# A four-direction scan and a layer of routed experts on one core: the steps beside a scan are split between the two ends of its turn, and the experts' tiles run in one stretch in the scheduler's order

## The chip, the cores and the metric

The kernel runs on one core of a Trainium2 chip. The metric is the device time of one execution in microseconds; the lower, the better. It was run three times before the change. One further execution was recorded by the hardware profiler, and all durations of single instructions come from that one. PE is the TensorE matmul unit, DVE VectorE, ACT ScalarE, POOL GpSimd and SP the engine that issues most of the DMAs.

## The reference, cut to what matters

Four images of 256 channels and 32x32 pixels pass through two layers. Each layer is a mixer and a layer of experts. The first layer (attention, then eight experts that all see every token) is not concerned here. The second layer is:

```python
# mixer: a selective scan in four directions, 16 states per channel
delta = softplus(xn @ W_delta + b_delta)          # xn: layer norm of the features
dA    = exp(delta[..., None] * -exp(A_log))       # decay per channel and state
dBx   = (delta * xn)[..., None] * (xn @ W_B)      # input per channel and state
h[l]  = dA[l] * h[l - 1] + dBx[l]                 # along rows forth, rows back, columns forth, columns back
y     = sum over states of h * (xn @ W_C), + xn * D, added to x; mean of the directions

# experts: a layer norm, a router, the best 2 of 8 experts for every token
logits = xn @ Wr + br;  top 2, softmax of the two
out    = x + sum of the two: w * (gelu((xn * ln_g[e] + ln_b[e]) @ W1[e] + b1[e]) @ W2[e] + b2[e])
```

There are 4 x 1024 tokens, so 8192 rows for the experts (each token goes to two), and the hidden size of an expert is 1024.

## The kernel before, in words

Tensors of the mixer lie as 128 channels (partitions) by 1024 pixels, two such halves for an image. The scan of one image, one half and one of 16 states is a unit; there are 128 of them, in the order image, half, state. A function `turn(k)` writes out, by hand, the instructions of one turn, which serves several units at different points of their way; inside a manual schedule, each engine gets its instructions in the order in which the code issues them. In turn k:

- at its beginning `for step in steps: next(step, None)` runs one step of the side work (below);
- for unit k+2 SP issues the loads of two broadcast rows (`rows`);
- for unit k+1 ACT computes the decays along the columns (L1514); when that unit is the first of a half, DVE first runs a running sum `cum` over delta (L1609), from which ACT makes `prod` (`products`);
- for unit k-1 POOL multiplies `prod` by the incoming column state (L1560, writes `da_c`), and PE adds that;
- for unit k DVE scans along the rows forth (L1540) and back (L1549), each over 128x1024; PE adds both into a sum in PSUM (`hp`, L1535); POOL takes a small difference `gap`;
- ACT computes the row decays of unit k+1 (L1522), POOL its inputs `uu` (L1527);
- if there is one, POOL issues an indirect DMA that sends 128 tokens to their places for the experts (L1288);
- DVE multiplies the two halves of unit k-1's sum by a row (`yc`, L1576), PE adds them into y, and the last state of a half adds y to x (L1580);
- DVE runs a short scan `come` of 32 steps (L1555);
- a second `for step in steps: next(step, None)` runs another step of the side work;
- DVE scans along the columns (L1566), PE adds.

The side work is written as generators, which stop at each `yield`. `Prep.steps()` prepares the next image: layer norm (L1400 on), the products with W_B and W_C, and for each of four quarters the softplus (L1481 to L1489: `sp`, with ACT's exponentials and logarithms in between) and `rest` (L1457, L1458: delta times the input, and the part with D). `norm(b)` and `route(b)` compute the experts' layer norm, the router's logits, the best two experts, and the place of every token among its expert's rows; `scatter(b)` then sends the tokens (L1288). A turn takes a step at its beginning and one at its end, so the number of `yield`s between two groups of instructions decides at which of the two a group falls. In the kernel before the groups with VectorE work fall at a turn's beginning.

The first three images are routed beside the scans. The last one, image 3, is known only when the scans have ended, so its routing runs beside the experts. There, `Tile` is the work on 256 rows of one expert: `slots` loads the rows (L1665), `weights` loads W1, W2, the biases and the layer norm's factors (L1670 to L1680), `inputs` transposes on PE (`tp`, L1688), scales on DVE (`xe`, L1691) and computes the places of the results (`to`, L1694, a pool of 8 buffers), `hidden` is the first matmul (`hp`, L1703) with ACT's Gelu (`hid`, L1705), `result` the second (`yp`, L1711), a bias on DVE (`ys`, L1714) and two indirect DMAs from POOL that put the rows where they belong (L1716). The 17 `early` tiles are full of rows of the first three images. Their order is written by hand in a manual schedule, with the routing of image 3 in between (`beside`); `hp` and `yp` have two PSUM buffers each. The other tiles are `late`: 19 as a rule, in the scheduler's order, with three `hp` and two `yp` buffers. More of them are written into a branch ahead of these 19, taken only when the counts need it (L1771); in the profiled execution it is not taken. At the end the two results of each token are read back, weighted, transposed and added to x (L1783 to L1795).

Of the kernel before, what the change touches and what calls it, by code (L numbers as in the profile page):

```python
# [11 lines left out]
F32 = mybir.dt.float32  # L12
# [9 lines left out]
P = 128  # L22
# [36 lines left out]
def metaformer(ctx: ExitStack, tc: tile.TileContext, t: dict, out: bass.AP):  # L59
# [1129 lines left out]
    def route(b, space, psum, tag):  # L1189

        used = 0
        yield
# [35 lines left out]
        yield  # L1228
        flat = both.rearrange("p n e -> p (n e)")
# [7 lines left out]
        nc.vector.tensor_copy(place, sums[:, 0].rearrange("p n e -> p e n"))  # L1237
        nc.vector.tensor_scalar(m1, m2, 1.0, None, ALU.add)
# [4 lines left out]
        yield  # L1243
        yield
# [48 lines left out]
    def norm(b, pool, psum, tag, raw_tag, d):  # L1293
# [32 lines left out]
        def rsqrt(dst):  # L1326

            nc.scalar.activation(sd, ve, AF.Sqrt)
            yield
            yield  # L1330
            nc.vector.reciprocal(r0, sd)
            nc.vector.tensor_tensor(sd, r0, r0, ALU.mult)
            nc.vector.tensor_tensor(sd, sd, ve, ALU.mult)
            nc.vector.tensor_scalar(sd, sd, -0.5, 1.5, ALU.mult, ALU.add)
            nc.vector.tensor_tensor(dst, r0, sd, ALU.mult)


        yield
# [7 lines left out]
        nc.vector.tensor_tensor(s2, s2, s1, ALU.mult)  # L1346
        for n in range(NT):
            nc.scalar.mul(tok[:, n, :C], tok[:, n, :C], s2[:, n : n + 1])
# [3 lines left out]
    with ExitStack() as st:  # L1352
# [34 lines left out]
        class Prep:  # L1387
# [9 lines left out]
            def steps(self):  # L1397
# [28 lines left out]
                yield  # L1426
# [4 lines left out]
                nc.vector.tensor_tensor(rs, r0, rr, ALU.mult)  # L1431
                yield
# [29 lines left out]
                for c in range(CT):  # L1462
                    for h in range(NHALF):
                        cols = ts(h, HALF)
                        zp = ps_m.tile([P, HALF], F32, tag="hp", name="zp")
                        for k in range(CT):
                            nc.tensor.matmul(zp, wd[:, k, ts(c, P)], xm[:, k, cols],
                                             start=(k == 0), stop=(k == CT - 1))
                        yield
                        dd = self.delta[:, c, cols]  # L1470
                        sp = p1.tile([P, 4 * HALF], F32, tag="sp", name="sp")
                        v, up, ln, ru = (sp[:, ts(i, HALF)] for i in range(4))
                        nc.scalar.activation(dd, zp, AF.Relu, bias=bd[:, c : c + 1])
                        nc.scalar.activation(v, zp, AF.Abs, bias=bd[:, c : c + 1])
                        nc.scalar.activation(v, v, AF.Exp, scale=-1.0)
                        if last is not None:
                            rest(*last)
                        last = c, cols
                        yield
                        yield  # L1480
                        nc.vector.tensor_scalar(up, v, 1.0, None, ALU.add)  # L1481
                        nc.scalar.activation(ln, up, AF.Ln)
                        nc.scalar.activation(ru, ln, AF.Exp, scale=-1.0)
                        nc.vector.scalar_tensor_tensor(v, up, 1.0, v, ALU.subtract, ALU.subtract, reverse1=True)
                        yield
                        yield
                        nc.vector.tensor_tensor(v, v, ru, ALU.mult)
                        nc.vector.tensor_tensor(v, v, ln, ALU.add)
                        nc.vector.tensor_tensor(dd, dd, v, ALU.add)  # L1489
                        yield  # L1490
                yield
                rest(*last)
# [103 lines left out]
        def turn(k):  # L1596
# [52 lines left out]
    with ExitStack() as st:  # L1649
# [70 lines left out]
        with ExitStack() as sa:  # L1720
# [3 lines left out]
            ps_h = sa.enter_context(tc.tile_pool(name="m1_ps_h", bufs=2, space=PSUM))  # L1724
            ps_y = sa.enter_context(tc.tile_pool(name="m1_ps_y", bufs=2, space=PSUM))
            with tc.manual_schedule():
                todo = [Tile(early, i, "xa", EARLY) for i in range(EARLY)]
                for i in range(EARLY):
                    todo[i].slots()
                    if i < 2:  # L1730
                        todo[i].weights()
                b = B - 1
                routing = chain(norm(b, pa, psa, "t", "raw", pa.tile([P, CT, L], F32, tag="nm_d", name="nm_d")),
                                route(b, pa.tile([P, NUMBERS], F32, tag="numbers", name="numbers"), psa, "t"))
                sending = scatter(b)

                def beside():
                    for _ in range(2):
                        if next(routing, "end") == "end":
                            next(sending, None)  # L1740

                next(routing)
                todo[0].inputs(ps_t)
                for i in range(EARLY):
# [8 lines left out]
                for _ in chain(routing, sending):  # L1753
                    pass

        def run(which):
            with ExitStack() as sb:
                ps_t = sb.enter_context(tc.tile_pool(name="m1_ps_t", bufs=2, space=PSUM))
                ps_h = sb.enter_context(tc.tile_pool(name="m1_ps_h", bufs=3, space=PSUM))
                ps_y = sb.enter_context(tc.tile_pool(name="m1_ps_y", bufs=2, space=PSUM))  # L1760
                for i in which:
                    one_tile = Tile(late, i)
                    one_tile.weights()
                    one_tile.slots()
                    one_tile.inputs(ps_t)
                    one_tile.hidden(ps_h)
                    one_tile.result(ps_y)

        more_tiles = nc.values_load(extra[0:1, 0:1], min_val=0, max_val=1,
                                    skip_runtime_bounds_check_because="a comparison gives 0 or 1")  # L1770
# [96 lines left out]
```

## Time and profile before

| what | us |
|---|---|
| three runs | 4603.13, 4604.02, 4629.91; median 4604.02 |
| the profiled execution | 4608.16 |
| its span, from the first to the last instruction | 4606.1 |
| attention and the first experts | 0 to 2505 |
| preparation of the first image | 2505 to 2557 |
| the scans, 128 turns | 2557 to 3905; DVE busy 1243.3, PE 1247.3, ACT 917.2, POOL 639.6 |
| early tiles, 17 | 3905 to 4251; PE busy 287.8, DVE 46.6 |
| between early and late tiles | 4251 to 4263; PE busy 0.8 |
| late tiles, 19 | 4263 to 4556; PE busy 278.0, DVE 33.7 |
| the last sums | 4556 to 4606; PE busy 15.8, DVE 24.1 |

The page gives each engine's busy time, and under it one digit for each fortieth of the span, the busy share in tenths. A group's row names line, engine, operation, output and input with their shapes and the number of instructions; after the first bar come busy time (us) and the mean of one (ns), after the second the idle time of the engine just before them and what ended most of it. In a timeline the columns are start, duration, engine, line and operation; a bracket tells how long the engine was idle before and what released it. A row of waits names the waiting group, what ended the wait, then the sum in us, the number and the longest. An instruction that was started but could not proceed counts as busy, so a contended operation shows as a long one and not as a wait.

### The profile page before, as it was taken

Reading aid. Unit: us, or ns where it says so; the run is one execution under the profiler, and the core shown is the slowest. Engines: PE = TensorE matmul, PEld = TensorE weight load, DVE = VectorE, ACT = ScalarE, POOL = GpSimd, SP = SyncE. Lnnn points to the kernel's source line nnn. Section 1 sums busy time; section 2 is a strip of 40 time slices with the busy share of each in tenths; the row PEclk is TensorE's granted clock in tenths of the full one; section 3 lists DMA queues with packets and bytes.
Section 4 is the critical chain, followed back from the end, with each engine's and each line's share of the span. In section 5 each row is a group of like instructions: output and inputs, shape, how many; then the busy total and the mean of one; then the engine's idle time right before and its main releaser. Section 6 shows DMA issues by size and latency. Waiting matters only on the chain. (4 is left out here: it accounts for less than half of the span.)

```text
span 4606.1 us, 51252 instructions
## 1 busy us (share of the span) xinstructions
PE 3933.2 (85%) x18522; PEld 2160.5 (47%) x18522; DVE 3137.6 (68%) x5121; ACT 2887.2 (63%) x3788; POOL 1632.1 (35%) x1257
## 2 busy tenths in 40 slices
PE   7478878887888887689999789999999989887996
PEld 4143434443444443366665333433433434666785
DVE  3788899898989898422223799899899898110112
ACT  3989999999899899231112676767767755221222
POOL 0255445555554555310000344445445445011110
PEclk9568877887788788879999899999999999899997
DMA  9200000000000000100000223223333334444555
GB/s 288 56 1 1 10 1 1 1 10 1 1 1 10 1 1 10 38 1 0 0 1 11 84 97 110 101 97 113 102 98 112 104 103 122 150 147 129 184 182 183
DMA packets 171770, 306.81 MB, mean 67 GB/s; under 512 B 27753, under 2 KB 116594, under 8 KB 171506
## 3 DMA queue, kind: packets, MB, share of 16 engines
q1 hardware_dynamic: 161184, 284.10, 19.7%
q0 software_dynamic: 6528, 17.90, 1.0%
q8 instruction: 150, 2.46, 0.2%
q10 hardware_dynamic: 3794, 1.42, 0.1%
q14 instruction: 114, 0.93, 0.1%
HBM read 246.68 MB, written 56.69 MB: 66 GB/s over the span
## 5 line engine op out<-in xcount | busy, mean ns | idle before, releaser
L543 POOL TENSOR_SCALAR dr<-s_n,last 128x1024 bf16<-128x1024 f32 x256 | 728.8, 2864 | 882.3 <-DVE state L571 379.4
L459 ACT ACTIVATE junk_a<-s_n,state 128x1024 int8<-128x1024 f32 x448 | 514.6, 1149 | 23.9 <-DVE state L577 8.2
L1705 ACT ACTIVATE hid<-hp,b 128x256 f32<-128x256 f32 x288 | 134.2, 474 | 466.2 <-PE hp L1703 461.6
L463 DVE TENSOR_SCALAR_CACHE_REDUCE junk_v<-s_n,state 128x1024 int8<-128x1024 f32 x320 | 408.7, 1277 | 8.8
L1560 POOL TENSOR_TENSOR da_c<-prod,come 128x1024 f32<-128x1024 f32 x128 | 261.5, 2043 | 412.7 <-DVE h L1566 362.4
L1114 DVE SCALAR_TENSOR_TENSOR acc<-y,tk_comb,acc 128x256 f32<-128x256 f32 x256 | 120.9, 484 | 349.7 <-PE y L1112 344.1
L510 DVE SCALAR_TENSOR_TENSOR w<-s_n,win 128x1024 f32<-128x1024 f32 x256 | 349.6, 1366 | 5.2
L1703 PE MATMUL hp<-xe,w 128*128 128x256 f32 x1152 | 291.1, 403 | 65.2 <-ACT hid L1705 44.6
L1535 PE MATMUL hp<-h,twice 128*128 128x512 f32 x512 | 253.2, 618 | 91.0 <-DVE h L1540 90.8
L611 ACT ACTIVATE ex<-sT 128x1024 f32<-128x1024 f32 x256 | 247.0, 1015 | 122.5 <-PE sT L603 122.4
L513 DVE MAX8 win<-w 128x8 f32<-128x1024 f32 x256 | 314.5, 1228 | 8.9
L1527 POOL TENSOR_TENSOR uu<-dx,bb 128x1024 f32<-128x1024 f32 x128 | 304.2, 2377 | 40.5 <-DVE dx L1457 40.5
L1107 ACT ACTIVATE hid<-hp,b 128x512 f32<-128x512 f32 x128 | 88.0, 688 | 345.5 <-PE hp L1105 344.7
L459 ACT ACTIVATE junk_a<-s_n,guess 128x1024 int8<-128x1024 f32 x256 | 294.1, 1149 | 7.4
L621 PE MATMUL o_ps<-ex,vT 128*32 128x256 f32 x2048 | 249.8, 458 | 51.5 <-ACT ex L611 41.1
L1540 DVE TENSOR_TENSOR_SCAN h<-da,uu 128x1024 f32<-128x1024 f32 x128 | 291.2, 2275 | 2.7 <-ACT da L1522 2.7
L1566 DVE TENSOR_TENSOR_SCAN h<-da_c,uu 128x1024 f32<-128x1024 f32 x128 | 289.8, 2264 | 0.0
L1549 DVE TENSOR_TENSOR_SCAN h<-da,uu 128x1024 f32<-128x1024 f32 x128 | 289.6, 2262 | 0.0
L1703 PEld LDWEIGHTS hp<-xe,w 128*128 128x128 f32 x1152 | 217.7, 198 | 132.5 <-ACT hid L1705 77.3
L1522 ACT ACTIVATE da<-delta,a_log 128x1024 f32<-128x1024 f32 x128 | 142.8, 1115 | 211.4 <-DVE h L1549 211.4
L1514 ACT ACTIVATE da_c<-delta,a_log 128x1024 f32<-128x1024 f32 x128 | 268.3, 2096 | 0.1
L1112 PE MATMUL y<-w,hid 128*128 128x256 f32 x1024 | 262.9, 394 | 0.0
(517 smaller groups left out, 8209.5 us busy)
## 6 DMA issues: line engine op xcount, KB each, us to landing
bb<-bc_d SPq DMA_DIRECT2D x128, 512.0 KB, 5.0
cb<-bc_d SPq DMA_DIRECT2D x128, 512.0 KB, 4.2
w<-in_w SPq DMA_DIRECT2D x36, 1024.0 KB, 5.1
w2e<-in_w SPq DMA_DIRECT2D x36, 1024.0 KB, 5.6
slots_x<-zeros SPq DMA_DIRECT2D x1, 33282.0 KB, 128.4
y<-results SPq DMA_DIRECT2D x8, 1024.0 KB, 7.2
xs<-slots_x SPq DMA_DIRECT2D x19, 258.0 KB, 5.6
b2e<-in_b SPq DMA_DIRECT2D x36, 128.0 KB, 5.4
```

The costliest lines, as they stand in the source:

```text
L459: nc.scalar.activation(junk, self.row(r), AF.Sign, bias=thr, scale=-1.0, accum_out=u)
L463: nc.vector.tensor_scalar(junk, self.row(r), thr, None, ALU.is_lt, ALU.add, accum_out=u)
L510: nc.vector.scalar_tensor_tensor(w, self.row(r), self.win[:, r, 0:1], self.row(r), ALU.is_gt if r < LAST_DVE else ALU.is_ge, ALU.subtract, ...
L513: nc.vector.max(out=self.win[:, r, 1:], in_=w)
L543: ins = nc.gpsimd.tensor_scalar(dr, self.row(r), self.last[:, r : r + 1], None, ALU.is_lt)
L1112: nc.tensor.matmul(y, hid[:, f, ts(i, P)], w2[:, e, f, :], start=(f == 0), stop=(f == CT - 1))
L1514: nc.scalar.activation(grid(self.da_c), cols_flipped(self.prep.delta[:, self.c]), AF.Exp, scale=self.decay)
L1527: nc.gpsimd.tensor_tensor(self.uu[:, 0], self.prep.dx[:, self.c], self.bb, ALU.mult)
L1540: nc.vector.tensor_tensor_scan(rows.rearrange("p r w -> p (r w)"), self.da, self.uu[:, 0], 0.0, ALU.mult, ALU.add)
L1549: nc.vector.tensor_tensor_scan(hs[:, ::-1], self.da[:, ::-1], self.uu[:, 0][:, ::-1], 0.0, ALU.mult, ALU.add)
L1566: nc.vector.tensor_tensor_scan(hs, self.da_c, self.uu[:, 1], 0.0, ALU.mult, ALU.add)
L1703: nc.tensor.matmul(hp[:, f % 2], self.w1[:, c, ts(f, P)], self.xe[:, c], start=(c == 0), stop=(c == CT - 1))
```

## The change

Three things are done.

1. In the side work, `yield`s are moved, so that VectorE's steps with both inputs in SBUF fall at the end of a turn and those that read PSUM at its beginning. `rest` of a quarter follows the next quarter's matmuls at once.
2. The running sum `cum` of a half is issued one turn earlier, after the second step of a turn and ahead of its columns scan.
3. Early and late tiles are in one stretch without a manual schedule: each early tile is `inputs`, `hidden`, `result`, with six steps of the routing of image 3 after it (the routing and its scatter as one chain), and the scheduler sets the order. `hp` has three buffers, `yp` one. The branch with more late tiles stands after the 19, no longer ahead of them.

```diff
     def route(b, space, psum, tag):
         used = 0
-        yield
...
         nc.vector.tensor_tensor(both, hot1, hot2, ALU.add)
         yield
+        yield
...
         nc.vector.tensor_copy(place, sums[:, 0].rearrange("p n e -> p e n"))
+        yield
         nc.vector.tensor_scalar(m1, m2, 1.0, None, ALU.add)
...
         nc.vector.memset(keep[:, :, 0:1], 0.0)
-        yield
-        yield
         nc.vector.tensor_tensor_scan(cum.rearrange("p e n -> p (e n)"), keep.rearrange("p e n -> p (e n)"),
...
         def rsqrt(dst):
+            yield
             nc.scalar.activation(sd, ve, AF.Sqrt)
-            yield
             yield
...
-        yield
         nc.vector.tensor_scalar(ve, var, 1e-5, None, ALU.add)
...
         nc.vector.tensor_tensor(s2, s2, s1, ALU.mult)
+        yield
         for n in range(NT):
...
                 nc.scalar.activation(sd, ve, AF.Sqrt)
                 yield
-                yield
                 nc.vector.reciprocal(r0, sd)
...
                 nc.vector.tensor_tensor(rs, r0, rr, ALU.mult)
+                yield
                 yield
...
+                        if last is not None:
+                            rest(*last)
+                        last = c, cols
                         yield
...
                         nc.scalar.activation(v, v, AF.Exp, scale=-1.0)
-                        if last is not None:
-                            rest(*last)
-                        last = c, cols
-                        yield
                         yield
                         nc.vector.tensor_scalar(up, v, 1.0, None, ALU.add)
+                        nc.vector.scalar_tensor_tensor(v, up, 1.0, v, ALU.subtract, ALU.subtract, reverse1=True)
+                        yield
                         nc.scalar.activation(ln, up, AF.Ln)
                         nc.scalar.activation(ru, ln, AF.Exp, scale=-1.0)
-                        nc.vector.scalar_tensor_tensor(v, up, 1.0, v, ALU.subtract, ALU.subtract, reverse1=True)
-                        yield
                         yield
                         nc.vector.tensor_tensor(v, v, ru, ALU.mult)
                         nc.vector.tensor_tensor(v, v, ln, ALU.add)
                         nc.vector.tensor_tensor(dd, dd, v, ALU.add)
                         yield
+                        yield
+                rest(*last)
                 yield
-                rest(*last)
                 yield
...
             if 0 <= k + 1 < len(order):
-                b, c, s = order[k + 1]
-                if s == 0:
-
-                    cum = p1.tile([P, L], F32, tag="cum", name="cum", bufs=2)
-                    nc.vector.tensor_tensor_scan(cum, inner, preps[b].delta[:, c], 0.0, ALU.mult, ALU.add)
                 scans[k + 1].column_decays()
...
                 for step in steps:
                     next(step, None)
+            if 0 <= k + 2 < len(order) and order[k + 2][2] == 0:
+
+                b, c, _ = order[k + 2]
+                cum = p1.tile([P, L], F32, tag="cum", name="cum", bufs=2)
+                nc.vector.tensor_tensor_scan(cum, inner, preps[b].delta[:, c], 0.0, ALU.mult, ALU.add)
+            if 0 <= k < len(order):
                 scans[k].columns()
...
-            ps_h = sa.enter_context(tc.tile_pool(name="m1_ps_h", bufs=2, space=PSUM))
-            ps_y = sa.enter_context(tc.tile_pool(name="m1_ps_y", bufs=2, space=PSUM))
-            with tc.manual_schedule():
...
-                next(routing)
-                todo[0].inputs(ps_t)
-                for i in range(EARLY):
-                    todo[i].hidden(ps_h)
-                    beside()
-                    if i + 1 < EARLY:
-                        todo[i + 1].inputs(ps_t)
-                    todo[i].result(ps_y)
-                    if i + 2 < EARLY:
-                        todo[i + 2].weights()
-                    beside()
...
-        with tc.If(more_tiles > 0):
-            run(range(USUAL - EARLY, NTILE - EARLY))
-        run(range(USUAL - EARLY))
+            ps_h = sa.enter_context(tc.tile_pool(name="m1_ps_h", bufs=3, space=PSUM))
+            ps_y = sa.enter_context(tc.tile_pool(name="m1_ps_y", bufs=1, space=PSUM))
+
+            def run(one_tile):
+                one_tile.inputs(ps_t)
+                one_tile.hidden(ps_h)
+                one_tile.result(ps_y)
...
+            for i in range(EARLY):
+                run(todo[i])
+                if i + 2 < EARLY:
+                    todo[i + 2].weights()
+                for _ in range(6):
+                    next(routing, None)
...
+            run_late(range(USUAL - EARLY))
...
+            with tc.If(more_tiles > 0):
+                run_late(range(USUAL - EARLY, NTILE - EARLY))
```

The lines after the change are nearly all one less than before (L1540 is L1539), `cum` is L1636, the branch L1758, and the last sums begin at L1769.

More of the change, by code (lines that the diff above doesn't have):

```diff
@@ L1723, in metaformer @@
             ps_t = sa.enter_context(tc.tile_pool(name="m1_ps_t", bufs=2, space=PSUM))
-            ps_h = sa.enter_context(tc.tile_pool(name="m1_ps_h", bufs=2, space=PSUM))
-            ps_y = sa.enter_context(tc.tile_pool(name="m1_ps_y", bufs=2, space=PSUM))
-            with tc.manual_schedule():
-                todo = [Tile(early, i, "xa", EARLY) for i in range(EARLY)]
-                for i in range(EARLY):
[L1729 to L1740, printed above, removed]
-                next(routing)
-                todo[0].inputs(ps_t)
-                for i in range(EARLY):
-                    todo[i].hidden(ps_h)
-                    beside()
-                    if i + 1 < EARLY:
-                        todo[i + 1].inputs(ps_t)
-                    todo[i].result(ps_y)
-                    if i + 2 < EARLY:
-                        todo[i + 2].weights()
-                    beside()
-                for _ in chain(routing, sending):
-                    pass
@@ L1756, in run @@
[L1756 to L1760, printed above, removed]
+            ps_h = sa.enter_context(tc.tile_pool(name="m1_ps_h", bufs=3, space=PSUM))
+            ps_y = sa.enter_context(tc.tile_pool(name="m1_ps_y", bufs=1, space=PSUM))
@@ new lines, in run @@
+            def run(one_tile):
+                one_tile.inputs(ps_t)
+                one_tile.hidden(ps_h)
+                one_tile.result(ps_y)
+            todo = [Tile(early, i, "xa", EARLY) for i in range(EARLY)]
+            for i in range(EARLY):
+                todo[i].slots()
+                if i < 2:
+                    todo[i].weights()
+            b = B - 1
+            routing = chain(norm(b, pa, psa, "t", "raw", pa.tile([P, CT, L], F32, tag="nm_d", name="nm_d")),
+                            route(b, pa.tile([P, NUMBERS], F32, tag="numbers", name="numbers"), psa, "t"), scatter(b))
@@ L1761, in run, with run_late @@
+            for i in range(EARLY):
+                run(todo[i])
[3 more added lines that the diff above has]
+                    next(routing, None)
+            assert next(routing, "end") == "end"
+            def run_late(which):
                 for i in which:
@@ L1764, in run @@
                     one_tile.slots()
[L1765 to L1770, printed above, removed]
-        with tc.If(more_tiles > 0):
-            run(range(USUAL - EARLY, NTILE - EARLY))
-        run(range(USUAL - EARLY))
+                    run(one_tile)
+            run_late(range(USUAL - EARLY))
+            more_tiles = nc.values_load(extra[0:1, 0:1], min_val=0, max_val=1,
+                                        skip_runtime_bounds_check_because="a comparison gives 0 or 1")
+            with tc.If(more_tiles > 0):
+                run_late(range(USUAL - EARLY, NTILE - EARLY))
         with ExitStack() as sc:
```

## The prediction

> **What bounds the kernel now.** I read the page's parts 1 and 2 first, then the busy time by stretches, then DVE's groups with shapes kept apart, the timeline of one turn, and PE's waits in the experts' stage.
>
> ```profile
> PE 3933.2 (85%) x18522; PEld 2160.5 (47%) x18522; DVE 3137.6 (68%) x5121; ACT 2887.2 (63%) x3788; POOL 1632.1 (35%) x1257
> PE   7478878887888887689999789999999989887996
> ...
> DVE  3788899898989898422223799899899898110112
> ```
>
> The averages mislead: a digit is 115 us, and by stretches the span falls into attention to 1900, the first experts to 2505, preparation to 2557, the scans to 3905, the second experts to 4556 and the sums to 4606. No edit touches anything ahead of 2505, so 2505 us stay. In the scans DVE is busy 1243 of 1348 us and PE 1247: both look full. The rows tell which of them has slack in it (DVE, 2540 to 3905; after the bar the busy time and the mean ns of one):
>
> ```profile
> L1488 DVE TENSOR_TENSOR sp<-sp 128x512 f32<-128x512 f32 x15 | 29.7, 1980 | 0.5
> L1484 DVE SCALAR_TENSOR_TENSOR sp<-sp 128x512 f32<-128x512 f32 x15 | 29.5, 1964 | 0.5
> L1458 DVE SCALAR_TENSOR_TENSOR x<-xm,dskip,x 128x512 f32<-128x512 f32 x12 | 28.8, 2401 | 0.0
> L1487 DVE TENSOR_TENSOR sp<-sp 128x512 f32<-128x512 f32 x15 | 10.0, 665 | 4.7 <-ACT sp L1483 4.7
> ```
>
> L1487 and L1488 are the same operation on the same shape, 665 against 1980 ns. The timeline says why (start, us, engine):
>
> ```profile
> 2687.69 0.66 DVE L1487 TENSOR_TENSOR sp<-sp 128x512 f32<-128x512 f32 x1
> 2687.91 2.21 POOL L1560 TENSOR_TENSOR da_c<-prod,come 128x1024 f32<-128x1024 f32 x1 [3.15 <-DVE h L1566]
> 2688.38 2.29 DVE L1488 TENSOR_TENSOR sp<-sp 128x512 f32<-128x512 f32 x1
> 2690.71 0.69 DVE L1489 TENSOR_TENSOR delta<-delta,sp 128x512 f32<-128x512 f32 x1
> ```
>
> POOL's L1560 starts beside the step, L1488 begins at 2688.38 and ends only after L1560 has ended; L1489, with POOL done, takes 0.69. So the busy time of DVE holds hidden waits.
>
> [...] after a 3.48 us idle, three groups of eight matmuls at 4012.9 to 4026 took 3.78 us instead of 1.99, while after 11.2 us of idle only about 2 us were slow.
>
> **The change, part by part: scans.** A turn on DVE is: first call of the step, forth scan, back scan, two output products, the short scan, second call, columns scan. Start to start an empty turn takes 2.18+2.18+1.18+0.13+2.18 = 7.85 us. L1560 starts 0.1 to 0.2 us after the columns scan, so the first call stands exactly beside it; the second call starts 5.6 us into the turn, when POOL's product L1527 (done by about 4.95) is over and POOL waits for the columns scan. In before all step work falls into the first call. The order of instructions of the changed kernel has the SBUF-only work in the second call, the PSUM readers (L1304, L1317, L1408, L1421, L1441, L1236, L1237) in the first. Removed, as excess over the uncontended duration:
> - per quarter of a preparation L1488 1.60 (2.29−0.69), L1484 1.59, L1458 1.71; 12 quarters run inside turns: 12 × 4.90 = 58.8 us;
> - routing: L1333 6×1.60 = 9.6, L1209 8.6, L1247 5.1, L1257 4.4, L1238 2.9, L1429 1.6, L1168 1.3: 33.5 us.
>
> Together 92.3. What comes back: a quarter's three turns took 10.78+10.51+11.50 = 32.79 and fall to 27.89; PE needs 5 groups of 4 half-matmuls a turn, 8.58 us, and 1.72 for the quarter's zp: 27.46 in three turns. DVE still sets the pace, but with 0.4 us to spare. I charge 4 us for turns where PE becomes the bound (the row of waits already has yc on PE's hp with 18.3 us), 4 us for the PSUM readers of two routed batches that now wait for PE (1.2+0.55+0.15 for a batch, twice), and 1.3 for the layer norm's first factor. The scan cum (L1609, about 2.2 us, 8 times) is only moved, to the second call; DVE pays the same, and ACT's products no longer wait for it, which is off the path (ACT fills 6.3 of 7.85 us). The step's DMA of bc keeps its place; the two row loads per turn on SP too. Net **83 us** (bounds 65: PE binds in most heavy turns; 92: nothing comes back).
>
> **Experts.** Before, an early tile waits four times for ACT, since hp has two buffers; a late tile, with three, does not (PE's waits, us, count, longest; then PE's timeline):
>
> ```profile
> PE hp L1703 <- ACT hid L1705: 44.6, 68, 3.5
> PE hp L1703 <- DVE xe L1691: 20.0, 19, 5.6
> PE tp L1688 <- DMA xs<-slots_x: 11.2, 1, 11.2
> ```
>
> ```profile
> 4182.58 1.99 PE L1703 MATMUL hp<-xe,w 128*128 128x256 f32 x8 [0.61 <-ACT hid L1705]
> ...
> 4281.47 7.17 PE L1703 MATMUL hp<-xe,w 128*128 128x256 f32 x32 [0.80 <-DVE xe L1691]
> ```
>
> A steady early tile takes 17.63 us, a late one 15.33 (hp 7.19, yp 6.92, tp 0.43, wait 0.80). After, hp has three buffers everywhere, and the order shows two tiles' tp together, so one wait for two tiles: 14.95. The 11.2 us for xs, when SP's first late loads stood behind the branch, go too: those loads need only the last slot scatter, long landed by then.
>
> But the scheduler's order adds a wait. `to` (8 buffers) of tile i waits until the result scatters of tile i−8 have landed, and on DVE to(12) now stands ahead of ys(5), xe(6), xe(7); to(13) ahead of ys(6); to(14) ahead of ys(7), xe(8), xe(9). PE waits for these. The scatters wait for each other on POOL and are mixed with batch 3's 16 slot scatters, which become ready after tile 3:
>
> ```profile
> 4120.36 0.96 POOL L1288 DMA_INDIRECT slots_x<-tok,slot  x1 [0.30 <-issue]
> 4125.13 0.96 POOL L1288 DMA_INDIRECT slots_x<-tok,slot  x1 [3.80 <-DMA slots_x<-tok,slot]
> 4128.35 0.96 POOL L1288 DMA_INDIRECT slots_x<-tok,slot  x1 [2.26 <-DMA slots_x<-tok,slot]
> ```
>
> From 4120.36 to 4162.59 there are 13 steps of both kinds, 3.25 us each. With T3 the end of tile 3's yp, the first slot is ready about 7 us later (estimate from the durations of the routing's small operations), and landing takes 3.7. Tile 4's second result is the 8th of that chain and lands at T3+33.5, tile 5's (16th) at T3+59.5, tile 6's (22nd) at T3+7+21×3.25+3.7 = T3+79. Tile 8 can start about 1.7 us later, at T3+80.7, against 4×14.95 = 59.8 unhindered: a loss of 21 us, in three stalls of about 5, 5 and 11. They may bring half rate; a spell cost 3×1.79 = 5.4, and I take one and a half, 8 us. T3 comes at 4000 (in before's time), 8.4 ahead of its 4008.4, by 16 waits of 0.56 less a little. So the late tiles start at 4000+80.7+9×14.95+8 = 4223, against 4262.4: 39. Late tiles gain 2.5 (no slow start), and the branch, now behind them, costs the last sums' first load about 3 (its read waits for POOL's queue, 2.15 us before). Net **39 us** (bounds: 64 with no stall; 0).
>
> **Sum.** 83+39 = 122 from the span of 4606.1 gives 4484; the profiled execution, 4608.2, gives 4486. The median, 4604.0, lies 4.2 below that execution, so 4482.
>
> **Rivals.**
> - A, 0.17: the `to` wait does not bite, for slots are ready sooner or chain faster: 4604−83−64 = 4457. For: steps of 1.26 occur where kinds alternate. Against: the slot-to-slot steps are 2.3 to 7.3.
> - B, 0.17: the chain goes at the slots' own mean of 4.4, not 3.25. Tile 8 starts 24 us later and two more slow spells add 11: experts gain about 4, time 4517.
> - C, 0.10: PE sets the heavy turns, since 0.4 us in three turns is little and a group late by more than about 1.6 us stops the products: half the scan gain, 4604−42−39 = 4523.
> - D, 0.03, the change doesn't do what it says: second-call work meets POOL too (L1527 or a scatter runs late), scans as before: 4565.
> - E, 0.03, slower: the chain of scatters paces the experts. Late start is 4155+21s for a step of s; it eats both gains from 4345 on, s = 9.0 us. With s = 10 it ends at about 4625. Even the slowest step seen, 7.25, stays below.
>
> My forecast has 0.50, its own range 4468 to 4503. The range 4445 to 4530 takes in A, B and C. About 1% (46 us) is what a measurement of this kernel can tell from no change: only D, E and tails of B and C come near: faster 0.93, same 0.05, slower 0.02.
>
> **What would show it.** Right: L1488 and L1484 near 0.69, L1458 near 0.69, L1333 near 0.17; scan stage about 1265 us; yc's wait for hp up by a few us; no ACT wait of hp, no 11.2 us for xs; hp or yp waiting three times in tiles 6 to 8 for DVE, whose `to` waited for a result scatter. Wrong: L1488 still at 2 us (D), heavy turns at 9.5 with yc waiting (C), no pause in tiles 6 to 8 (A) or pauses over 35 us (B). If ACT turned up ahead of the scans, I would have misjudged its margin.

## The result, and the profile after

Four executions of the changed kernel took 4463.87 to 4474.22 us, median 4469.62; of the kernel before, measured beside it, 4603.13 to 4629.91, median 4610.62. The ratio is 0.9687, with a 95% interval of 0.9652 to 0.9723. The profiled execution has a span of 4472.0 us, 134.1 less than before's 4606.1. The page after, its parts 1 and 2:

```profile
PE 3892.6 (87%) x18522; PEld 2166.2 (48%) x18522; DVE 3046.6 (68%) x5121; ACT 2884.8 (65%) x3790; POOL 1613.6 (36%) x1257
PE   8378878887888788689999799999999999979996
...
DVE  2788898889988998722222489989999999411112
```

DVE executes the same 5121 instructions in 91.0 us less: the waits that hid in its busy time. PE's row has nines where the experts had eights.

A whole-span difference mixes three things, so I cut both executions at the same instructions: the first forth scan, the first matmul of the experts' stage (`nm_mean` after the last scan), the first transpose of a late tile, the end of the last `yp`.

| stretch, us | before | after | difference |
|---|---|---|---|
| to the first forth scan | 2556.8 | 2562.0 | +5.2 |
| the scans | 1347.8 | 1276.0 | −71.8 |
| experts, to the first late tile | 357.8 | 290.4 | −67.4 |
| late tiles | 293.8 | 291.8 | −2.0 |
| last sums | 49.9 | 51.8 | +1.9 |

In the first row, the first 2505 us are code that no edit touches, and the preparation of the first image, whose steps are only reordered, takes 48.5 to 49.7 us in every kernel. Over all kernels below the row lies between 2542.6 and 2564.4, so it carries much of the spread of the medians; the scans' stretch with one and the same code lies within 3 us. Stretches are compared below wherever a few microseconds matter. (The table's −2.0 and +1.9 are of that size too.)

DVE's groups in the scans, after (L1486, L1485, L1480 and L1457 were L1488, L1487, L1484 and L1458; mean ns after the comma):

```profile
L1486 DVE TENSOR_TENSOR sp<-sp 128x512 f32<-128x512 f32 x16 | 11.3, 704 | 0.5
L1485 DVE TENSOR_TENSOR sp<-sp 128x512 f32<-128x512 f32 x16 | 10.8, 672 | 8.6 <-ACT sp L1483 8.6
L1480 DVE SCALAR_TENSOR_TENSOR sp<-sp 128x512 f32<-128x512 f32 x15 | 10.4, 692 | 0.5
L1457 DVE SCALAR_TENSOR_TENSOR x<-xm,dskip,x 128x512 f32<-128x512 f32 x12 | 8.9, 746 | 0.0
```

In L1486, L1480 and L1457, 1980, 1964 and 2401 ns have become 704, 692 and 746. The timeline of one turn shows the place (of DVE and POOL only, and some lines left out):

```profile
3163.01 2.37 POOL L1526 TENSOR_TENSOR uu<-dx,bb 128x1024 f32<-128x1024 f32 x1
...
3165.53 1.01 POOL L1287 DMA_INDIRECT slots_x<-tok,slot  x1 [0.15 <-issue]
...
3166.12 0.67 DVE L1485 TENSOR_TENSOR sp<-sp 128x512 f32<-128x512 f32 x1
...
3166.82 0.69 DVE L1486 TENSOR_TENSOR sp<-sp 128x512 f32<-128x512 f32 x1
...
3167.55 0.69 DVE L1487 TENSOR_TENSOR delta<-delta,sp 128x512 f32<-128x512 f32 x1
...
3168.16 2.29 DVE L1565 TENSOR_TENSOR_SCAN h<-da_c,uu 128x1024 f32<-128x1024 f32 x1
...
3170.62 1.90 POOL L1559 TENSOR_TENSOR da_c<-prod,come 128x1024 f32<-128x1024 f32 x1 [4.09 <-DVE h L1565]
```

POOL's product is over at 3165.38 and the next begins at 3170.62; the three steps fit between. POOL only issues an indirect DMA there, beside which L1485 still takes 0.67. What now stands beside POOL's L1559 reads PSUM, and is not longer there:

```profile
2967.65 1.91 POOL L1559 TENSOR_TENSOR da_c<-prod,come 128x1024 f32<-128x1024 f32 x1 [4.82 <-DVE h L1565]
2968.99 1.28 DVE L1407 TENSOR_TENSOR xm<-x,ln_mean 128x512 f32<-128x512 f32 x2 [1.51 <-PE ln_mean L1404]
```

The first of the two L1407 starts 0.57 us before POOL is done, and both together take 1.28, as they do in the kernel before with no product of POOL beside them (L1408 at 2977.45, 1.28). The trace of the kernel before has a pair of this kind beside the product too, L1441, with one input in SBUF and one in PSUM:

```profile
2627.02 1.92 POOL L1560 TENSOR_TENSOR da_c<-prod,come 128x1024 f32<-128x1024 f32 x1 [3.16 <-DVE h L1566]
2628.06 1.29 DVE L1441 TENSOR_TENSOR xm<-xm,ln_rb 128x512 f32<-128x512 f32 x2 [1.19 <-PE ln_rb L1437]
```

All twelve L1441 of the scans take 679 to 687 ns each, those beside the product among them, where L1488 took 2.29 us beside it.

In the experts' stage, PE's waits after:

```profile
PE hp L1703 <- DVE xe L1691: 39.1, 27, 13.3
...
PE yp L1711 <- DVE ys L1714: 3.3, 1, 3.3
```

The 44.6 us for ACT and the 11.2 for xs are gone, and the predicted wait has come: PE's timeline (first fence) and DVE's (second).

```profile
3948.29 9.08 PE L1703 MATMUL hp<-xe,w 128*128 128x256 f32 x32 [7.37 <-DVE xe L1691]
...
3974.48 7.17 PE L1711 MATMUL yp<-w2e,hid 128*128 128x256 f32 x32 [3.28 <-DVE ys L1714]
...
3995.86 9.18 PE L1703 MATMUL hp<-xe,w 128*128 128x256 f32 x32 [13.33 <-DVE xe L1691]
```

```profile
3946.96 0.22 DVE L1694 SCALAR_TENSOR_TENSOR to<-xa,early_expert 128x2 int32<-128x2 f32 x1 [20.01 <-DMA results<-ys,to]
3947.10 0.69 DVE L1714 TENSOR_TENSOR ys<-yp,b2e 128x512 f32<-128x512 f32 x1
3947.70 1.89 DVE L1691 TENSOR_SCALAR xe<-tp,lng,lnb 128x256 f32<-128x256 f32 x4
...
3994.53 0.22 DVE L1694 SCALAR_TENSOR_TENSOR to<-xa,early_expert 128x2 int32<-128x2 f32 x1 [20.11 <-DMA results<-ys,to]
```

Tiles 6, 7 and 8 wait 7.4, 3.3 and 13.3 us. A 0.22 us instruction, `to`, stands 20 us for a scatter of results, with `ys` and `xe` behind it. Row "PE waits for DVE xe" names only the last link; DVE's own bracket names the DMA.

### The profile page after: what moved, and what is told of

It is laid out like the page before. It is cut to its first block, busy times and chain, and to the rows that moved or that the text cites. A ratio compares the mean times of both kernels' runs of the same rounds, so it can differ in the third digit from the quotient of the medians.

```text
span 4472.0 us, 51207 instructions
## 1 busy us (share of the span) xinstructions
PE 3892.6 (87%) x18522; PEld 2166.2 (48%) x18522; DVE 3046.6 (68%) x5121; ACT 2884.8 (65%) x3790; POOL 1613.6 (36%) x1257
## 4 chain that ended last, share of the span: by engine, by line
PE 40%; DVE 10%; issue 3%; DMA 2%; POOL 1%; ACT 1%; DVEq 0%; SPq 0%; ACTq 0%; POOLq 0%
PE hp L1534 9%; PE hp L1703 6%; PE y L1112 5%; PE yp L1711 5%; PE hp L1105 5%; PE y L1576 3%; PE hp L1569 3%; DVE h L1548 2%; DVE h L1539 2%; DVE h L1565 2%; DVE yc L1575 1%; POOL da_c L1559 1%; DMA y<-results 1%; PE y L183 1%; PE zp L1466 0%
## 5 line engine op out<-in xcount | busy, mean ns | idle before, releaser
L1559 POOL TENSOR_TENSOR da_c<-prod,come 128x1024 f32<-128x1024 f32 x128 | 244.7, 1911 | 529.7 <-DVE h L1565 467.1
L1703 PE MATMUL hp<-xe,w 128*128 128x256 f32 x1152 | 263.9, 386 | 39.4 <-DVE xe L1691 39.1
L1539 DVE TENSOR_TENSOR_SCAN h<-da,uu 128x1024 f32<-128x1024 f32 x128 | 290.6, 2270 | 2.7 <-ACT da L1521 2.7
L621 PE MATMUL o_ps<-ex,vT 128*32 128x256 f32 x2048 | 248.0, 457 | 50.7 <-ACT ex L611 39.6
L1569 PE MATMUL hp<-h,ident 128*128 128x512 f32 x512 | 254.4, 620 | 32.4 <-DVE h L1565 31.6
L1711 PE MATMUL yp<-w2e,hid 128*128 128x256 f32 x1152 | 256.0, 379 | 4.9 <-DVE ys L1714 3.3
```

Of the source, the lines that this page charges most:

```text
L1539: nc.vector.tensor_tensor_scan(rows.rearrange("p r w -> p (r w)"), self.da, self.uu[:, 0], 0.0, ALU.mult, ALU.add)
L1569: nc.tensor.matmul(cols_flipped(self.hp[h]), ident, grid(hs)[:, :, ts(h, half)], start=False, stop=False)
L1703: nc.tensor.matmul(hp[:, f % 2], self.w1[:, c, ts(f, P)], self.xe[:, c], start=(c == 0), stop=(c == CT - 1))
L1711: nc.tensor.matmul(yp[:, a], self.hid[:, f, ts(a, P)], self.w2[:, f, :], start=(f == 0), stop=(f == NF - 1))
```

## The experiments

Medians are over at least four executions, taken beside the kernel before on the same chip; two kernels have one execution, the profiled one, and are judged by its stretches.

**The scans' part alone.** The experts' stage is that of before.

> The first two parts of the change alone (the yields and cum); the experts' stage is that of before. Theory (the two parts add up[...]): about 72 us less than before, 4532, with the scans' stretch at 1276 from the first forth scan to the experts' first matmul, and the experts' stage at before's 701.5. Rival (part of the scans' gain is lent by the experts' stage, or the reverse): the time is more than 10 us off 4532.

Measured: 4530.1 against 4607.0, ratio 0.984 (0.9801 to 0.9879); scans 1278.8, experts and sums 693.4 (before 701.5). The last 8.1 us were not expected. What they come from was not shown.

**The experts' part alone,** with before's scans and routing.

> The third part alone, with before's scans. Theory: about 67 us less than before, 4537; the experts' stage at 634, with three waits of PE in tiles 6, 7 and 8 behind a to that waits for a result scatter. Rival (the moved yields in the routing of image 3 are what let the experts' stage start faster): the stage is over 645, as the routing's steps fall otherwise.

Measured: 4531.8 against 4607.0, ratio 0.984 (0.9808 to 0.9873); scans 1347.2, experts and sums 628.9, image 3's sums at 71.8 us from the stage's start (after 72.4), longest wait for xe 10.1. The scans' gain comes from the first two parts alone, the experts' from the third, within some 5 us each, and in the scheduler's order the moved yields of the routing do nothing for the experts. The stage is 5 us shorter than in the changed kernel's profile; in three later kernels with the same stage it is 627.5 to 629.3, so 634.0 was a long one, by its waits for xe, ys and hid (44.0 us against 39.6 here).

**More buffers for `to`.**

```diff
-                self.to = pb.tile([P, T // P], I32, tag="to", name="to", bufs=8)
+                self.to = pb.tile([P, T // P], I32, tag="to", name="to", bufs=EARLY + 3)
```

> The changed kernel with 20 buffers for to instead of 8; nothing else. Theory (DVE stands in a to that waits for the result scatters of eight tiles before, and PE behind it): the waits of 7.4, 3.3 and 13.3 us go, and with them about 4 us of slow matmuls: 28 us less, 4442. Rival 1 (the chain of scatters itself is the limit, the wait moves to ys, which has 4 buffers and waits for the same scatters): 15 us or more of it stay. Rival 2 (the pauses are for other work on DVE): nothing changes.

Measured: 4436.1, ratio to before 0.9641 (0.9607 to 0.9676), experts and sums 603.0. That is 31.0 less than in the changed kernel's profile, which was a long one, and 24 to 26 less than in the three kernels with the same stage. PE's waits:

```profile
PE hp L1703 <- DVE xe L1691: 19.3, 27, 1.0
```

The longest falls from 13.3 to 1.0; 27 short ones remain. The wait was for `to`'s buffer alone, neither for the chain as such nor for other work on DVE.

**Half of zp's matmuls left out.**

```diff
-                        for k in range(CT):
-                            nc.tensor.matmul(zp, wd[:, k, ts(c, P)], xm[:, k, cols],
-                                             start=(k == 0), stop=(k == CT - 1))
+                        nc.tensor.matmul(zp, wd[:, c, ts(c, P)], xm[:, c, cols], start=True, stop=True)
```

> The changed kernel with half of the matmuls of zp left out (one of the two halves of the input channels; the output is then not the reference's). Theory (PE binds in the heavy turns, where zp's 1.72 us delay the column sums): the turns with L1480 fall from 9.41 to 8.95, the scans' stretch by 5 to 10 us. Rival (the 0.46 us are DVE's own or ACT's): these turns stay at 9.4.

Measured in one profiled execution: scans 1268.3, 7.7 less. A turn with L1480 (from one forth scan to the next) fell from 9.41 to 8.92, eight times; turns 10, 15 and 16 by 0.9, 0.6 and 1.6. So PE was the bound there: with its matmuls thinned, three heavy turns take 9.91+9.12+8.92 = 27.95, the 27.89 that I had worked out for DVE. These are 6.9 us. The rest is not shown to be zp's: turn 33, which has no zp, is 1.3 shorter, but such a turn takes about 12.5 or 11.2 us without any edit (before: turn 33 12.47, turn 65 11.18, turn 97 12.46). The remaining differences cancel but for 0.5.

**The mirror of the yields.** One yield more at the start of `steps` and of `routed`.

```diff
                 b = self.b
+                yield
...
             nonlocal sending
+            yield
             yield from norm(b, p1, ps_m, "hp", "hp", p1.tile([P, CT, L], F32, tag="xm", name="nm_d"))
```

> The changed kernel with one yield more at the beginning of each image's preparation and of each routing: the same groups of instructions, each half a turn later, so that those with both inputs in SBUF stand at a turn's beginning, beside POOL's product, and those that read PSUM at its end. Theory (the place beside POOL costs): L1480, L1486 and L1457 are back at 1.9 to 2.4 us, and the scans lose 55 us or more of their 72. Rival (the regrouping, with fewer or fuller steps, makes the gain): the time stays within 20 us of the changed kernel's.

Measured: 4617.7 against 4606.5, ratio 1.0024 (1.001 to 1.0037); scans 1432.5, 156 more than the changed kernel, 85 more than before. DVE's groups and waits (lines of this kernel are one more than after's):

```profile
L1458 DVE SCALAR_TENSOR_TENSOR x<-xm,dskip,x 128x512 f32<-128x512 f32 x12 | 28.8, 2404 | 0.0
L1481 DVE SCALAR_TENSOR_TENSOR sp<-sp 128x512 f32<-128x512 f32 x16 | 17.4, 1090 | 0.5
L1208 DVE TENSOR_TENSOR numbers<-lg,numbers 128x64 f32<-128x64 f32 x6 | 10.0, 1672 | 0.2
```

```profile
DVE yc L1576 <- PE hp L1535: 108.4, 114, 6.0
...
DVE sp L1486 <- ACT sp L1484: 19.1, 9, 3.5
DVE sp L1480 <- ACT sp L1478: 11.0, 8, 1.4
```

Beside POOL the contended durations are back: L1458 at 2.40, L1208 at 1.67. L1481 is only partly so, at 1.09 in the mean, and its mean hides the clearest test of all: four of the sixteen start while POOL's product runs and take 2.28 us, the other twelve meet none and take 0.69. The sign is the expected one and the size is more than expected. But only 73 of the 156 us are longer instructions (DVE busy 1228.6 us in the scans, 1155.8 in the changed kernel); the other 84 are DVE's waits. The mirror also puts the matmuls that feed PSUM readers elsewhere in PE's order, and `yc` waits 108.4 us for PE instead of 23.2 in the same part of the scans. It shows that the regrouping isn't the gain; it does not measure the place beside POOL by itself.

**`cum` back at its old place,** all else as changed.

```diff
             if 0 <= k + 1 < len(order):
+                b, c, s = order[k + 1]
+                if s == 0:
+                    cum = p1.tile([P, L], F32, tag="cum", name="cum", bufs=2)
+                    nc.vector.tensor_tensor_scan(cum, inner, preps[b].delta[:, c], 0.0, ALU.mult, ALU.add)
                 scans[k + 1].column_decays()
...
-            if 0 <= k + 2 < len(order) and order[k + 2][2] == 0:
...
```

> The changed kernel with cum back at its old place, behind the columns scan of the turn before and the first step. Theory (cum is only moved, its cost is the same and ACT's products have time): the scans' stretch stays at 1276, within 3 us. Rival (products and POOL's L1559 come late behind cum, and DVE's scan behind them): 5 to 15 us more.

Measured in one profiled execution: scans 1270.4, 5.6 less than the changed kernel. Neither theory had it on this side: moving `cum` costs. By turns: 15, 16 and 17 are 0.6, 1.1 and 0.9 shorter, turn 112 by 1.1, and turns 32, 48, 64, 80 and 96 by 0.35 each, in most of which DVE waits for PE's `y`, `hp` or `nm_mean`. Turn 33 is 1.3 shorter too, but that is the turn with two values, and before has the long one with `cum` at the same old place; without it some 4 us are left, where the scans of one and the same code differ by up to 2.8. Standing ahead of the columns scan, `cum` puts its 2.2 us ahead of the columns' matmuls; behind that scan it did not. This fits, and was not tested by itself.

**Three buffers for hp, in the order by hand.**

```diff
-            ps_h = sa.enter_context(tc.tile_pool(name="m1_ps_h", bufs=2, space=PSUM))
-            ps_y = sa.enter_context(tc.tile_pool(name="m1_ps_y", bufs=2, space=PSUM))
+            ps_h = sa.enter_context(tc.tile_pool(name="m1_ps_h", bufs=3, space=PSUM))
+            ps_y = sa.enter_context(tc.tile_pool(name="m1_ps_y", bufs=1, space=PSUM))
```

> The kernel before with three buffers for hp and one for yp in the early tiles; the order written by hand stays, as do the scans and the branch. Theory A (the early tiles lose by the buffers): the waits of hp for ACT, 44.6 us, go nearly all, about 40 us less than before: 4564. Theory B (the order by hand is what costs, the routing's matmuls standing between the tiles'): 15 us or less.

Measured: 4604.5 against 4606.5, ratio 1.000 (0.9987 to 1.0014). PE's waits:

```profile
PE hp L1703 <- ACT hid L1705: 44.6, 68, 3.5
```

Not one wait has gone. So the buffers were not the cause of what the prediction read from this row. B's number is right, its reason was still open.

**The branch last,** in the kernel before.

```diff
+        run(range(USUAL - EARLY))
         more_tiles = nc.values_load(extra[0:1, 0:1], min_val=0, max_val=1,
...
         with tc.If(more_tiles > 0):
             run(range(USUAL - EARLY, NTILE - EARLY))
-        run(range(USUAL - EARLY))
```

> The kernel before with the branch moved behind the 19 late tiles, and nothing else. Theory: the 11.2 us wait for xs goes, the last sums begin about 2 us later: 8 to 9 us less, 4595. Rival (the late tiles' first loads wait for something else, such as the last slot scatter or a buffer of the early tiles): 3 us or less.

Measured: 4591.3 against 4606.5, ratio 0.9971 (0.9959 to 0.9983, so 8 to 19 us less); experts and sums 693.4, 8.1 less; the 11.2 us row is gone.

**Order by hand, three buffers, branch last, the changed scans.** The edits of the last two, on the scans' part alone.

> The changed kernel's scans, and the experts in the order by hand with three buffers for hp, one for yp, and the branch last. Theory (buffers and branch make the experts' gain, the scheduler's order gives what its to waits take back): about 4470, as the changed kernel. Rival (the scheduler's order itself is worth 20 us or more, for it puts the routing's work beside matmuls): about 4490.

Measured: 4513.4, ratio 0.9806 (0.9775 to 0.9837), experts and sums 679.9. The rival, and beyond: here the scheduler's order is worth 46 to 52 us, against the 634.0 of the changed kernel's profile or the 628 to 629 of its siblings.

**The matmuls of a pair first,** in the kernel before. The code by hand issues the matmuls of block f, its Gelu, then block f+1, and both blocks lie in one hp tile.

```diff
-                for f in range(NF):
-                    if f % 2 == 0:
-                        hp = ps_h.tile([P, 2, T], F32, tag="hp", name="hp")
-                    for c in range(CT):
-                        nc.tensor.matmul(hp[:, f % 2], ...)
-                    nc.scalar.activation(self.hid[:, f], hp[:, f % 2], ...)
+                for pair in range(NF // 2):
+                    hp = ps_h.tile([P, 2, T], F32, tag="hp", name="hp")
+                    for f in (2 * pair, 2 * pair + 1):
+                        for c in range(CT):
+                            nc.tensor.matmul(hp[:, f % 2], ...)
+                    for f in (2 * pair, 2 * pair + 1):
+                        nc.scalar.activation(self.hid[:, f], hp[:, f % 2], ...)
```

> The kernel before, with one thing changed in hidden(): the matmuls of both hidden blocks that share an hp tile come first, then both Gelus, instead of block by block. Three hp buffers had left the 68 waits of hp for ACT, 44.6 us, as they were. Theory (the second block of a pair waits for the first one's Gelu because both lie in one hp tile and the order is followed as written): the waits for ACT fall from 44.6 to under 10 us, the early tiles' period from 17.63 to about 15.4, and the time by 30 to 40 us: 4570. Rival (ACT itself is too slow for two blocks, so PE waits later, in yp or for the next hp): the period stays over 17.

Measured: 4529.2 against 4606.9, ratio 0.9833 (0.9814 to 0.9851); experts and sums 626.4, 75.1 less. PE's waits, then its timeline:

```profile
PE hp L1703 <- ACT hid L1706: 2.4, 3, 1.2
```

```profile
4028.90 7.07 PE L1703 MATMUL hp<-xe,w 128*128 128x256 f32 x32
4035.81 0.60 PE L1688 MATMUL tp<-ident,xa 128*128 128x128 f32 x4
4036.25 7.07 PE L1712 MATMUL yp<-w2e,hid 128*128 128x256 f32 x32
4043.16 7.07 PE L1703 MATMUL hp<-xe,w 128*128 128x256 f32 x32
```

The period is 14.26, not 17.63. Of the 3.37 us, 2.3 were the shown idle times (0.61 and three of 0.56); the other 1.07 is that each of the four groups behind a wait takes longer, those of eight 1.99 instead of 8/32 of 6.91, 1.73, which no wait row shows. Seventeen tiles make 57 of the 75 us. The rest, mostly ahead of image 3's sums (106.1 us from the start instead of 139.9), fits the clock: before the first late tile one group of 16 matmuls takes 5.32 us instead of 3.72, so PE works some 3.3 us at half its clock, where in the kernel before it works 36.4 us at a granted clock of 0.50. That is worth about 16.5 us (an estimate, half of the difference). The theory was right and its size half of the truth. The runs do not tell whether the shared tile counts or the stretch of PSUM that it fills.

**The same edit with the changed scans, three buffers and the branch last.**

> The changed kernel's scans, the experts in the order by hand with three hp buffers, one yp, the branch last, and the matmuls of a pair first (679.9 us for experts and sums without this last edit). Theory (what the scheduler's order gave was to take the second block past the first one's Gelu): the stage falls by 35 to 45 to about 640, as the changed kernel's 634. Rival (it gave also a fuller start, with the routing's work beside matmuls): the stage stays over 655, with the sums of image 3 still at 125 us or more after the stage's beginning instead of 72.

Measured: 4446.4, ratio 0.9654 (0.9634 to 0.9673); experts and sums 613.3, sums of image 3 at 107.5. Both expected too long a stage. The order by hand, without the wait inside a pair, is 20.7 us shorter than the changed kernel's stage (15 shorter than that stage in its siblings), and 10.3 longer than the scheduler's with more `to` buffers (603.0). The rival's one point holds: the scheduler's order starts the stage more densely, with the sums 35 us earlier.

**Late tiles' inputs one tile ahead,** with the 20 `to` buffers.

```diff
-                    run(one_tile)
+                    one_tile.inputs(ps_t)
+                    if ahead is not None:
+                        ahead.result(ps_y)
+                    one_tile.hidden(ps_h)
+                    ahead = one_tile
+                ahead.result(ps_y)
```

> The changed kernel with 20 buffers for to, and in the late tiles the inputs of the next tile before the result of this one. Theory (a late tile loses 0.80 us to the wait for xe, since tp is followed at once by hp): 19 times 0.80, so 15 us less than with the buffers alone: 4421, and the late tiles at 277 instead of 291.8. Rival (xs or the weights come late when tp is pulled forward, with two buffers each): the late tiles stay at 290 or more.

Measured: 4424.5, ratio 0.9608 (0.959 to 0.9626), late tiles 280.7, experts and sums 593.4. 11 of the 15 us come; PE's waits for xe are 5.4 us in all, and 3.1 us for xs on DMA are new, the rival's part. It is the fastest version that was run, with a ratio to before of 0.9608 where the changed kernel has 0.9687. Its combination with `cum` at its old place was not run.

## Why the prediction was right, and where its steps were off

- **Time.** 4482 stood against 4469.6, within the likeliest case's own range, 4468 to 4503. The main mechanisms held, but so close a sum is partly luck: the scans gained 11 us less than forecast (71.8, not 83) and the experts 28 more (67.5, not 39), and the two errors cancel in part.
- **The steps beside POOL.** Shown: L1486, L1480 and L1457 fell to 704, 692 and 746 ns, about their uncontended durations, and those that start behind POOL's product in the mirror are long again (2.28 us). That the readers of PSUM would stay short in their place was the author's assumption; L1407 beside the product, two in 1.28 us, bears it out. Why the steps on SBUF are long there was not shown.
- **What comes back.** The removal was right: the named operations together lost 91.5 us in the scans, 92.3 were forecast. 9.3 us were charged against it, but 20.5 are missing (92.3−71.8). DVE's idle time in the scans rose by 15.7 of them, from 104.5 to 120.2 us. The PSUM readers of two routed images were put at 4; the sixteen turns with them gained 13.2 where 20.4 were removed, so 7.2. `cum` was put at nothing, covered by ACT's margin; it seems to cost some 4, through PE, a cover that the step did not look at. PE as the bound was put at 4 for the heavy turns: with half of zp the eight turns with L1480 gave back 3.9, so this was right, but turns 10, 15 and 16 gave back 3.0 more. These figures are of single executions and share turns 15 and 16, so they don't add up to a full account.
- **The `to` wait.** Right in place, order and size: 21 us in three stalls of 5, 5 and 11 were predicted, 24.0 in 7.4, 3.3 and 13.3 measured; the chain went at 3.49 us a step (73.3 us for 21) instead of 3.25. Half rate was put at 8 us; the two hp groups behind the long pauses took 9.08 and 9.18 instead of 7.09, so 4.1. Taking the buffers' limit away gave 24 to 31.
- **Where the experts' 28 us more came from.** 39 was predicted, 67.5 measured. The step that failed is "T3 comes at 4000, 8.4 ahead, by 16 waits of 0.56": T3 was carried over from before, with its slow start. Image 3's sums, right behind T3, stand 72.4 us from the stage's start, not 95.4. The windows from the stage's start to T3, before and after (start and end, length, busy time and count of PE, PEld, DVE, ACT, POOL, granted clock, DMA's share, GB/s), show both halves:

```profile
3904.60:4008.40 103.80, 79.70 (x334) 60.56 (x333) 11.90 (x28) 23.93 (x55) 5.82 (x6) 0.88 0.53 169
```

```profile
3838.04:3910.50 72.46, 67.65 (x332) 56.55 (x331) 17.37 (x68) 33.09 (x70) 5.80 (x6) 1.00 0.75 242
```

About the same matmuls are busy 12 us less, at a granted clock of 1.00 instead of 0.88, and PE is idle 4.8 instead of 24.1 us. PE's longest pause there is 1.6 us instead of 5.6, and no stretch at half rate begins. Over the whole way to the first late tile PE works 8.0 us at a granted clock of 0.50 instead of 36.4; that is some 14 of the 67.4 us (an estimate, half of the difference), beside 38 of idle time. From T3 to the late tiles 223.3 was predicted and 218.0 measured, and the last terms (late tiles 2.5, branch 3) came at 2.0 and 1.9.
- **A right number by a wrong cause.** "Since hp has two buffers" is refuted: three change nothing. The waits came from the order by hand, in which the second block of a pair stood behind the Gelu of the first in the same tile (44.6 us of waits became 2.4 when both were written first). The predicted gain held because it used the two periods as measured, and the scheduler's order did remove the wait. Had the change been three buffers alone, the same working would have missed by some 40 us.
- **Rivals.** A's mechanism is refuted as a forecast (the wait bites) though its time is near; the 64 us that it gives the experts should have been 68 by the prediction's own terms (39 and the stalls' 21 and 8). B's step of 4.4 was not seen (3.49). C is true of the heavy turns and costs some 7 us, not 41. D and E are excluded by the traces: L1486 takes 0.70 in the place of 1.98, and the chain of scatters goes at 3.49 us a step, far from 9.0.

## What to carry to other kernels

A busy engine may be waiting: compare the same operation with itself, and if its duration has two values (0.69 and 2.29 us here), look at what runs beside the long one; then move it to where that other engine idles, and into its place operations whose duration the trace shows unchanged there (here those with an input in PSUM, 0.68 us each). In an order written by hand, two halves of one PSUM tile with a reader between them made a wait that a third buffer did not cure (44.6 us with two and with three); both halves written first left 2.4. When a scheduler sets the order, look for small instructions that wait for a buffer far ahead of their use, with others behind them on the same engine (here `to`, 0.22 us long, stood for 20 us ahead of `ys` and `xe`): more buffers for that small tile alone took the stalls away here (20 instead of 8).

## What the runs showed of the hardware that was not expected

How long PE ran slowly after a pause was not told by the length of the pause in these runs. One of 13.33 us cost the next hp group 2.1 us (9.18 instead of 7.09); one of 11.2 us, in the kernel before, cost the next 2.05 (9.14), which took some 4 us at half rate (a granted clock of 0.50 from 4264.19 to 4268.20) and not the 2 that the prediction read. One of 3.48 us, in the kernel before, was followed by three groups at 3.78 instead of 1.99, 5.4 us in all; the same pause in the same place of the kernel with three hp buffers by one group only (3.68). PE's timeline in the two:

```profile
4012.88 3.78 PE L1703 MATMUL hp<-xe,w 128*128 128x256 f32 x8 [3.48 <-ACT hid L1705]
4017.22 3.78 PE L1703 MATMUL hp<-xe,w 128*128 128x256 f32 x8 [0.56 <-ACT hid L1705]
4021.57 3.78 PE L1703 MATMUL hp<-xe,w 128*128 128x256 f32 x8 [0.56 <-ACT hid L1705]
```

```profile
4010.61 3.68 PE L1703 MATMUL hp<-xe,w 128*128 128x256 f32 x8 [3.48 <-ACT hid L1705]
4014.86 1.99 PE L1703 MATMUL hp<-xe,w 128*128 128x256 f32 x8 [0.56 <-ACT hid L1705]
```

In the kernel before the granted clock was 0.50 from 4012.88 to 4025.35, over the three slow groups with the pauses of 0.56 us between them, and 1.00 from 4026.90 to 4034.30. Why one stretch ended after one group and the other after three was not shown; no run varied it by itself. The prediction's 8 us for half rate rested on the long stretch.
